# A graph-attention layer on one core: alphas, sums and scores moved one step behind what they need

## The chip, the core and the metric

One core of a Trainium2 chip runs the whole kernel, in one launch. The metric is the device time in microseconds (us), the median of three runs. One further execution was recorded by the hardware profiler; all rows, waits and durations below come from it. Engines are named as in the profile: PE (TensorE matmuls), PEld (TensorE weight loads), DVE (VectorE), ACT (ScalarE), POOL (GpSimd), SP (SyncE, which here only issues DMAs). An engine takes its instructions in the order of the program, and engines wait for each other on semaphores.

## What is computed

There are 12500 nodes with 128 channels and 400000 edges, sorted by their destination. Cut to what matters, and with eight heads of 16 + 16 channels:

```
h       = relu(layernorm(x))
message = (h @ w_src + b_src)[src] + (h @ w_dst)[dst]
rad     = silu(silu(edge_attr @ w1 + b1) @ w2 + b2) @ w3 + b3
message = message * edge_weight * rad
a, v    = heads of message @ w_sep + b_sep          # 8 heads, 16 alphas and 16 values each
score   = sum(smooth_leaky_relu(a) * alpha_dot)     # one number per edge and head
att     = softmax of score over the edges of one destination
out     = x + segment_sum(v * att, dst) @ w_proj + b_proj
```

## The kernel before

**Stages.** A first stage makes the node tables `t_src` and `t_dst` in DRAM (up to L289). The edge stage, `passes`, takes most of the time: 400 steps of 1000 edges, each in two sections of 500 (`f` = 0, 1), in four tiles of 125 edges each. While the last steps drain, and behind them, the sums of sections that share a node are combined (L1012 to L1103); a last stage applies `w_proj` (L1139 to L1192).

**The order is written by hand.** The edge stage stands under a manual schedule: an engine's instructions come in the order in which `step(k)` calls the helpers. One call of `step(k)` works on several steps at once. It starts loads for step k+3 and the gather for k+4, does the radial MLP for k+3 (`e_T`), k+2 (`mlp1`), k+1 (`mlp2`) and k (`mlp3`), makes message k, its alphas and (every second step) its scores, and, 12 steps later (`LAG = 12`, `c = k - LAG`), values and sums of step c. The softmax over eight steps (`softmax_up`, `softmax_down`, `softmax_exp`, `softmax_T`) lies between scores and values.

**The helpers, and their lines in the profile.**

- `gather(k)`: 8 indirect DMAs on POOL, each of which gathers the `t_src` rows of 125 edges into `gs` (L718). `gs` has four buffers, so that the gather for step k+4 waits until message k has read its buffer.
- `mlp3(k)`: PE `p3` (L758), then DVE makes `rad` twice (L761).
- `message(k, rads)`: PE transposes `gs` into `pm` (8 instructions, L770), adds the destinations' rows by a one-hot product (L775), then DVE multiplies by `rad` into `mT` (L779).
- `alphas(k, f)`: PE `pa` (L783), ACT `sl` (L785), DVE `al` (L787).
- `scores(k)`: PE `misc` from the four `al` of two steps (L794), ACT `Sp` (L797), a store to DRAM by SP (L799).
- `sums_begin(c)`: ACT copies the softmax weights into `pvx` (L847), DVE makes the one-hot `oh` (L851, L854).
- `values(c, f)`: PE `V` (L864), DVE `pvx` (L866).
- `sums(c)`: PE `misc` from `oh` and `pvx`, 8 matmuls into two halves of the partitions (L875), ACT copies it to `ob` (L879). `store_win` and `store` (L883, L887) send `ob` to DRAM.
- `mlp1` is L736 and L739, `mlp2` L744 and L746, `e_T` L728 and L730, `softmax_T` L838 and L840.

**PSUM buffers.** All eight banks are in use, most tiles have a single buffer: `misc` is shared by sums, scores, `softmax_T` and `prep_make`; `m1` by `e_T` and `mlp2`; `p3` (two banks) by `mlp1` and `mlp3`; `pa` by the two alphas; `V` by the two values; `pm` has two buffers. A matmul into such a tile waits until the reader of its last content is done.

**The order within a step**, for PE: L758, L770, L775, L864, L783, L864, L736, L744, L783, L875, L728, and every second step L794.

Of the kernel before, what the change touches and what calls it, by code (L numbers as in the profile page):

```python
# [49 lines left out]
PR = 2 * SEC  # L50
MP = 8
MQ = 2 * MP
LAG = 12
EP = 8


# [1 line left out]
def gnn_kernel(ctx: ExitStack, tc: tile.TileContext, a: dict, out: bass.AP):  # L58
# [585 lines left out]
    def passes(w1b, w2b, w3b, b12, w_s, b_s, tgt, far):  # L644
# [5 lines left out]
        with tc.tile_pool(name="wk2", bufs=2) as sp, tc.tile_pool(name="ps", bufs=1, space=PSUM) as pp, \  # L650
# [62 lines left out]
            def gather(k):  # L713
                gs = lp.tile([P, 8, C], F32, name="gs", bufs=4)
                idx, _ = prep[k // 16]
                for j in range(8):
                    t = k % 16 * 8 + j
                    nc.gpsimd.indirect_dma_start(  # L718
                        out=gs[:, j, :], out_offset=None, in_=t_src[:, :],
                        in_offset=bass.IndirectOffsetOnAxis(ap=idx[:, t:t + 1], axis=0))  # L720
                gath[k] = gs
# [10 lines left out]
            def mlp1(k):  # L732
                p1 = pp.tile([P, 2, BANK], F32, name="p3")
                for q in range(2):
                    s = slice(q * 2 * RAD, (q + 1) * 2 * RAD)
                    nc.tensor.matmul(p1[:, q, 0:2 * T], w1b[s, :], eTs[k][s, :],  # L736
                                     start=True, stop=True)
                h1s[k] = sp.tile([P, SEC], F32, name="h1")
                nc.scalar.activation(h1s[k].rearrange("p (q e) -> p q e", q=2), p1[:, :, 0:2 * T],  # L739
                                     AF.Silu, bias=b12[:, 0:1], scale=1.0)  # L740
# [13 lines left out]
            def mlp3(k):  # L754
                p3 = pp.tile([C, 2, BANK], F32, name="p3")
                for f in range(2):
                    s = slice(f * FC, (f + 1) * FC)
                    nc.tensor.matmul(p3[:, f, 0:SEC], w3b[s, :], h2s[k][s, :], start=True, stop=True)  # L758
                rads = [sp.tile([C, SEC], F32, name="rad", bufs=3) for _ in range(2)]
                for f in range(2):  # L760
                    nc.vector.scalar_tensor_tensor(rads[f], p3[:, f, 0:SEC], b3, w_g[k][:, f * SEC:(f + 1) * SEC],  # L761
                                                   op0=ALU.add, op1=ALU.mult)
                return rads

            def message(k, rads):
                gs = gath[k]
                pm = [pp.tile([C, SEC], F32, name="pm", bufs=2) for _ in range(2)]
                for f in range(2):
                    for t in range(TS):
                        nc.tensor.matmul(pm[f][:, t * T:(t + 1) * T], gs[:T, f * TS + t, :],  # L770
                                         ident[:T, :T], start=(t == 0), stop=False,
                                         is_transpose=True, skip_group_check=True)
                for f in range(2):
                    s = slice(f * W, (f + 1) * W)
                    nc.tensor.matmul(pm[f], md[k][s, :], ohT[k][s, :], start=False, stop=True,  # L775
                                     skip_group_check=True)
                mTs[k] = sp.tile([C, PR], F32, name="mT", bufs=LAG + 1)
                for f in range(2):
                    nc.vector.tensor_mul(mTs[k][:, f * SEC:(f + 1) * SEC], pm[f], rads[f])  # L779

            def alphas(k, f):
                pa = pp.tile([C, SEC], F32, name="pa")
                nc.tensor.matmul(pa, w_a, mTs[k][:, f * SEC:(f + 1) * SEC], start=True, stop=True)  # L783
                sl = sp.tile([C, SEC], F32, name="sl")
                nc.scalar.activation(sl, pa, AF.Silu, bias=b_a, scale=1.0)  # L785
                al = sp.tile([C, SEC], F32, name="al", bufs=6)
                nc.vector.scalar_tensor_tensor(al, pa, 0.25, sl, op0=ALU.mult, op1=ALU.add)  # L787
                als[2 * k + f] = al
# [46 lines left out]
            def softmax_T(m):  # L835
                pt = pp.tile([T, TS, P], F32, name="misc")
                for t in range(TS):
                    nc.tensor.transpose(pt[:, t, :], Ps[m][:, t * T:(t + 1) * T], ident)  # L838
                Pem[m] = sp.tile([T, TS, MQ, H], F32, name="Pem")
                nc.scalar.copy(Pem[m].rearrange("p t q h -> p t (q h)"), pt)  # L840


            def sums_begin(c):
                pvx[c] = sp.tile([T, 2, TS, ROW], F32, name="pvx")
                q = c % MP * 2
                for f in range(2):
                    nc.scalar.copy(pvx[c][:, f, :, C:ROW], Pem[c // MP][:, :, q + f, :])  # L847
                _, loc = prep[c // 16]
                ohs[c] = sp.tile([T, 8, W], F32, name="oh")
                t0 = c % 16 * 8  # L850
                nc.vector.tensor_tensor(  # L851
                    ohs[c][:, :, 0:W - 1], lane[:T, 0:W - 1].unsqueeze(1).to_broadcast([T, 8, W - 1]),
                    loc[:, t0:t0 + 8].unsqueeze(2).to_broadcast([T, 8, W - 1]), op=ALU.is_equal)
                nc.vector.tensor_tensor(  # L854
                    ohs[c][:, :, W - 1].rearrange("p (f t) -> p f t", f=2),
                    loc[:, t0:t0 + 8].rearrange("p (f t) -> p f t", f=2),
                    far[:T, 2 * c:2 * c + 2].unsqueeze(2).to_broadcast([T, 2, TS]), op=ALU.is_equal)
# [24 lines left out]
            def store_win(c):  # L882
                nc.sync.dma_start(out=win[c * P:(c + 1) * P, :], in_=accs[c])  # L883

            def store(c, f):
                at = nc.sync.value_load(base[0:1, f, c:c + 1])
                nc.sync.dma_start(out=agg[ds(at, W - 1), :], in_=accs[c][f * W:(f + 1) * W - 1, :])  # L887

            def has(k):
                return 0 <= k < NP  # L890
# [4 lines left out]
                load_e(0, i)  # L895
            def step(k):
                c = k - LAG
                if has(c - 1):
                    store_win(c - 1)
                    store(c - 1, 0)  # L900

                if k % 16 == 4 and has(k + 12):
                    prep_load((k + 12) // 16)
                if has(k + 3):
                    load_w(k + 3)
                    load_md(k + 3)
                if k % 2 and has(k + 3):
                    load_d((k + 3) // 2)
                g, r = divmod(k + 3, EP)
                if k >= -3 and r < EP - 1 and has((g + 1) * EP):  # L910
                    for i in ((0, 1) if r == 0 else (r + 1,)):
                        load_e(g + 1, i)
                if has(k + 4) and (k + 4) % MP == 0:
                    load_sm((k + 4) // MP)
                if has(c - 1):
                    store(c - 1, 1)
                if 0 <= 2 * k < NZ:
                    for i in range(2 * k, min(2 * k + 2, NZ)):
                        zero(i)
                if k % 16 == 8 and has(k + 8):  # L920
                    prep_make((k + 8) // 16)
                if has(k + 4):
                    gather(k + 4)
                if has(c):
                    sums_begin(c)
                if has(k):
                    message(k, mlp3(k))
                if has(c):
                    values(c, 0)
                if has(k):  # L930
                    alphas(k, 0)
                if has(c):
                    values(c, 1)
                if has(k + 2):
                    mlp1(k + 2)
                if has(k + 1):
                    mlp2(k + 1)
                    one_hot_T(k + 1)
                if has(k):
                    alphas(k, 1)  # L940
                if has(c):
                    sums(c)
                m, r = divmod(k, MP)
                if has(k - MP):
                    if r == 1:
                        softmax_up(m - 1)
                    elif r == 2:
                        softmax_down(m - 1)
                        softmax_exp(m - 1)
                    elif r == 3:  # L950
                        softmax_T(m - 1)
                if has(k + 3):
                    e_T(k + 3)
                if has(k) and k % 2 == 1:
                    scores(k)

            for k in range(-5, NP):
                step(k)
# [128 lines left out]
            assert NA == 3 * 4 * P and NE - NA == P // 2  # L1087
            for k in range(NP, NP + LAG + 2):
                step(k)
# [148 lines left out]
```

## Time and profile before

| what | value |
|---|---|
| median of three runs | 6562.58 us (6560.19 to 6575.51) |
| the profiled execution's own time | 6566.2 us |
| its span, first to last instruction | 6564.2 us |
| PE busy | 5066.2 us, 77% |
| POOL busy | 3111.5 us, 47% |
| DVE busy | 2887.1 us, 44% |
| ACT busy | 1785.1 us, 27% |
| mean granted PE clock | 0.873 of full speed |
| first and last L758 | 238.6 and 6296.1 us |
| moved by DMA | 783.25 MB, 119 GB/s over the span |

The 400 steps lie between the two L758 times; outside them are the node stage (about 240 us) and the end (about 270 us). Busy shares are means over work that alternates between two kinds of step, with and without scores, so that the gain or loss of a change is read from one pair of steps in the timeline, not from the shares. The ends of matmuls are modelled by the profiler; when a matmul's result was really there is seen from the instruction on another engine that waited for it.

### The profile page before, as it was taken

How to read it: one execution, taken by the hardware profiler on the slowest of the kernel's cores; microseconds unless marked ns; L12 is line 12 of the kernel's file. 1: busy time of each engine (PE TensorE's matmuls, PEld its weight loads, DVE VectorE, ACT ScalarE, POOL GpSimd, SP SyncE). 2: the span in 40 equal slices, each digit the busy share in tenths (PEclk: the TensorE clock that was granted, in tenths of full speed). 3: DMA queues.
4: the chain of work that ended last, by engine and by line, in shares of the span. 5: the costliest groups of instructions: out<-in, count | busy, mean ns of one | idle time of the engine just before them, and what ended most of it. 6: DMA issues, size and time to landing. Idle time of an engine off the chain costs nothing. (4 is left out here: it accounts for less than half of the span.)

```text
span 6564.2 us, 79188 instructions
## 1 busy us (share of the span) xinstructions
PE 5066.2 (77%) x26490; PEld 2665.6 (41%) x26490; DVE 2887.1 (44%) x5210; ACT 1785.1 (27%) x3797; POOL 3111.5 (47%) x3231
## 2 busy tenths in 40 slices
PE   3477878787878878788788787887887878888774
PEld 2234444444444444444444444444444444444453
DVE  4234444444444444444444444444444444444465
ACT  3122222222222222222222222222222222222221
POOL 0455555455554545544455454454554545545402
PEclk7688898898998989988888898898888989888885
DMA  3454444444444444444444444444444444444423
GB/s 124 135 144 119 124 119 115 125 117 121 121 122 118 121 119 119 124 117 115 123 120 121 119 116 121 122 115 120 121 117 122 119 120 121 124 119 118 114 60 123
DMA packets 884920, 783.25 MB, mean 119 GB/s; under 512 B 527255, under 2 KB 773279, under 8 KB 884250
## 3 DMA queue, kind: packets, MB, share of 16 engines
q1 hardware_dynamic: 778482, 560.72, 31.0%
q0 software_dynamic: 102816, 210.37, 13.6%
q10 hardware_dynamic: 3202, 6.99, 0.3%
q8 instruction: 212, 3.47, 0.2%
q14 instruction: 208, 1.70, 0.1%
HBM read 643.82 MB, written 134.27 MB: 119 GB/s over the span
## 5 line engine op out<-in xcount | busy, mean ns | idle before, releaser
L718 POOL DMA_INDIRECT gs<-t_src,idx x3200 | 3067.4, 959 | 3189.3 <-PE pm L770 1756.2
L787 DVE SCALAR_TENSOR_TENSOR al<-pa,sl 128x500 f32<-128x500 f32 x800 | 542.9, 679 | 1570.9 <-ACT sl L785 1022.1
L761 DVE SCALAR_TENSOR_TENSOR rad<-p,c_fc_b,w_b 128x500 f32<-128x500 f32 x800 | 553.6, 734 | 1389.4 <-PE p L758 1102.0
L783 PE MATMUL pa<-mT,c_w_a 128*128 128x500 f32 x1600 | 833.7, 603 | 256.8 <-DVE mT L779 248.1
L785 ACT ACTIVATE sl<-pa,c_b_a 128x500 f32<-128x500 f32 x800 | 541.4, 677 | 1789.4 <-PE pa L783 626.9
L864 PEld LDWEIGHTS V<-c_w_v,mT 128*125 128x125 f32 x6208 | 741.2, 188 | 634.8 <-issue 337.9
L864 PE MATMUL V<-c_w_v,mT 128*125 128x128 f32 x6208 | 891.3, 286 | 23.2 <-issue 1.1
L794 PE MATMUL misc<-al,w_s 128*32 128x500 f32 x1600 | 365.9, 986 | 539.5 <-ACT ob L879 525.3
L779 DVE TENSOR_TENSOR mT<-pm,rad 128x500 f32<-128x500 f32 x800 | 504.3, 672 | 280.1 <-PE pm L775 252.8
L758 PE MATMUL p<-h,w3b 64*128 64x500 f32 x1600 | 625.5, 870 | 0.0
L770 PEld LDWEIGHTS pm<-ident,gs 125*128 125x128 f32 x3200 | 430.1, 169 | 435.9 <-issue 435.9
L866 DVE TENSOR_TENSOR pvx<-V,Pem 125x512 f32<-125x512 f32 x776 | 528.9, 682 | 44.4 <-PE m L744 26.5
L770 PE MATMUL pm<-ident,gs 125*128 125x125 f32 x3200 | 533.6, 321 | 0.0
L875 PEld LDWEIGHTS misc<-pvx,oh 125*64 125x64 f32 x6400 | 365.5, 137 | 322.4 <-issue 279.7
L875 PE MATMUL misc<-pvx,oh 125*64 125x136 f32 x6400 | 473.0, 287 | 28.2 <-DVE pvx L866 27.6
L783 PEld LDWEIGHTS pa<-mT,c_w_a 128*128 128x128 f32 x1600 | 269.5, 191 | 500.6 <-DVE mT L779 287.4
L775 PE MATMUL pm<-ohT,md 64*128 64x500 f32 x1600 | 471.0, 656 | 0.1
L739 ACT ACTIVATE h<-p,b 128x500 f32<-128x500 f32 x400 | 270.5, 676 | 700.9 <-PE pa L783 157.2
L879 ACT COPY ob<-misc 128x136 f32<-128x136 f32 x400 | 108.7, 272 | 1292.5 <-remote 630.5
L744 PE MATMUL m<-h,w2b 128*128 128x500 f32 x800 | 449.6, 644 | 0.0
L728 PE MATMUL m<-ident,e_t 125*128 125x125 f32 x800 | 187.4, 319 | 204.4 <-ACT h L746 169.8
L746 ACT ACTIVATE h<-m,b 128x500 f32<-128x500 f32 x400 | 270.7, 677 | 223.4 <-PE m L744 55.0
(145 smaller groups left out, 3153.1 us busy)
## 6 DMA issues: line engine op xcount, KB each, us to landing
w_b<-in_edge_weight SPq DMA_DIRECT2D x400, 500.0 KB
d_b<-in_dst SPq DMA_DIRECT2D x400, 250.0 KB
gs<-t_src,idx POOLq DMA_INDIRECT x3200
e_t<-in_edge_attr SPq DMA_DIRECT2D x400, 125.0 KB
sc_d<-Sp SPq DMA_DIRECT2D x200, 250.0 KB
win<-ob SPq DMA_DIRECT2D x400, 68.0 KB
agg<-ob SPq DMA_DIRECT2D x800, 33.5 KB
md<-t_dst SPq DMA_DIRECT2D x800, 32.0 KB
```

The source lines that it names most:

```text
L718: nc.gpsimd.indirect_dma_start(out=gs[:, j, :], out_offset=None, in_=t_src[:, :], in_offset=bass.IndirectOffsetOnAxis(ap=idx[:, t:t + 1], ...
L758: nc.tensor.matmul(p3[:, f, 0:SEC], w3b[s, :], h2s[k][s, :], start=True, stop=True)
L761: nc.vector.scalar_tensor_tensor(rads[f], p3[:, f, 0:SEC], b3, w_g[k][:, f * SEC:(f + 1) * SEC], op0=ALU.add, op1=ALU.mult)
L770: nc.tensor.matmul(pm[f][:, t * T:(t + 1) * T], gs[:T, f * TS + t, :], ident[:T, :T], start=(t == 0), stop=False, is_transpose=True, skip_ ...
L775: nc.tensor.matmul(pm[f], md[k][s, :], ohT[k][s, :], start=False, stop=True, skip_group_check=True)
L779: nc.vector.tensor_mul(mTs[k][:, f * SEC:(f + 1) * SEC], pm[f], rads[f])
L783: nc.tensor.matmul(pa, w_a, mTs[k][:, f * SEC:(f + 1) * SEC], start=True, stop=True)
L785: nc.scalar.activation(sl, pa, AF.Silu, bias=b_a, scale=1.0)
L787: nc.vector.scalar_tensor_tensor(al, pa, 0.25, sl, op0=ALU.mult, op1=ALU.add)
L864: nc.tensor.matmul(V[:, t, :], mTs[c][:, o:o + T], w_v, start=True, stop=True)
L866: nc.vector.tensor_mul(pvx[c][:, f, :, 0:C].rearrange("p t (h k) -> p t h k", h=H), V.rearrange("p t (h k) -> p t h k", h=H), Pem[c // MP] ...
L875: nc.tensor.matmul(acc[f * W:(f + 1) * W, :], ohs[c][:, f * TS + t, :], pvx[c][:, f, t, :], start=(t == 0), stop=(t == TS - 1), skip_group ...
```

## The change

Values, sums, alphas and scores change their places in `step(k)`:

- `LAG` goes from 12 to 13: values of step c come 13 steps after its message. `mT` has `LAG + 1` buffers and so gets one more.
- `alphas(k - 1, f)` instead of `alphas(k, f)`; `scores(k - 1)` at the end of even steps instead of `scores(k)` at the end of odd ones. The softmax helpers run one step later.
- `sums(c - 1)` instead of `sums(c)`, and no longer near the end of the step but between the two alphas, right after the first. The stores of `ob` follow one step later (`c - 2`).
- `sums_begin` is split into `weights` (ACT) and `one_hot` (DVE); the latter moves from the start of the step to its end.
- The first `values` moves ahead of `message`, the second behind `mlp1`.

PE's order within a step becomes: L758, L864, L770, L775, L783, L875, L736, L864, L744, L783, L728, and L794 every second step (lines as before the change).

```diff
-LAG = 12
+LAG = 13
...
-            def sums_begin(c):
+            def weights(c):
                 pvx[c] = sp.tile([T, 2, TS, ROW], F32, name="pvx")
                 q = c % MP * 2
                 for f in range(2):
                     nc.scalar.copy(pvx[c][:, f, :, C:ROW], Pem[c // MP][:, :, q + f, :])
+
+            def one_hot(c):
                 _, loc = prep[c // 16]
                 ohs[c] = sp.tile([T, 8, W], F32, name="oh")
...
-                if has(c - 1):
-                    store_win(c - 1)
-                    store(c - 1, 0)
+                if has(c - 2):
+                    store_win(c - 2)
+                    store(c - 2, 0)
...
-                if has(c - 1):
-                    store(c - 1, 1)
+                if has(c - 2):
+                    store(c - 2, 1)
...
                 if has(k + 4):
                     gather(k + 4)
+
                 if has(c):
-                    sums_begin(c)
-                if has(k):
-                    message(k, mlp3(k))
+                    weights(c)
+                rads = mlp3(k) if has(k) else None
                 if has(c):
                     values(c, 0)
                 if has(k):
-                    alphas(k, 0)
+                    message(k, rads)
+                if has(k - 1):
+                    alphas(k - 1, 0)
+                if has(c - 1):
+                    sums(c - 1)
+                if has(k + 2):
+                    mlp1(k + 2)
                 if has(c):
                     values(c, 1)
-                if has(k + 2):
-                    mlp1(k + 2)
                 if has(k + 1):
                     mlp2(k + 1)
                     one_hot_T(k + 1)
-                if has(k):
-                    alphas(k, 1)
-                if has(c):
-                    sums(c)
+                if has(k - 1):
+                    alphas(k - 1, 1)
                 m, r = divmod(k, MP)
                 if has(k - MP):
-                    if r == 1:
+                    if r == 2:
                         softmax_up(m - 1)
-                    elif r == 2:
+                    elif r == 3:
                         softmax_down(m - 1)
                         softmax_exp(m - 1)
-                    elif r == 3:
+                    elif r == 4:
                         softmax_T(m - 1)
+                if has(c):
+                    one_hot(c)
                 if has(k + 3):
                     e_T(k + 3)
-                if has(k) and k % 2 == 1:
-                    scores(k)
+                if has(k - 1) and k % 2 == 0:
+                    scores(k - 1)
```

## The prediction

> **What bounds the kernel now.** I read the page first. No engine is full, and PE comes nearest:
>
> ```profile
> PE 5066.2 (77%) x26490; PEld 2665.6 (41%) x26490; DVE 2887.1 (44%) x5210; ACT 1785.1 (27%) x3797; POOL 3111.5 (47%) x3231
> ...
> L718 POOL DMA_INDIRECT gs<-t_src,idx x3200 | 3067.4, 959 | 3189.3 <-PE pm L770 1756.2
> ```
>
> Second, the waits of PE (total, times, longest):
>
> ```profile
> PE misc L794 <- ACT ob L879: 525.3, 144, 4.3
> PE pa L783 <- DVE mT L779: 248.1, 169, 19.2
> PE misc L838 <- ACT ob L879: 196.3, 49, 6.5
> PE m L728 <- ACT h L746: 169.8, 103, 8.9
> ```
>
> Three of the four come from this: scores and `softmax_T` wait for the copy of the sums out of `misc`, and alphas for the message of their own step. Third, the timeline of two steps (start, duration, engine, operation, [idle before]):
>
> ```profile
> 3004.23 1.90 PE L794 MATMUL misc<-al,w_s 128*32 128x500 f32 x8 [3.52 <-ACT ob L879]
> 3006.06 2.04 PE L758 MATMUL p<-h,w3b 64*128 64x500 f32 x4
> ...
> 3010.23 0.94 POOL L718 DMA_INDIRECT gs<-t_src,idx  x1 [8.16 <-PE pm L770]
> ...
> 3016.51 1.15 PE L875 MATMUL misc<-pvx,oh 125*64 125x136 f32 x16
> ...
> 3017.95 1.11 PE L758 MATMUL p<-h,w3b 64*128 64x500 f32 x4
> ...
> 3018.96 0.94 POOL L718 DMA_INDIRECT gs<-t_src,idx  x1 [0.30 <-issue]
> ...
> 3021.63 0.27 ACT L879 COPY ob<-misc 128x136 f32<-128x136 f32 x1 [4.34 <-PE pm L775]
> 3021.73 1.38 DVE L761 SCALAR_TENSOR_TENSOR rad<-p,c_fc_b,w_b 128x500 f32<-128x500 f32 x2 [3.06 <-PE pm L775]
> ...
> 3023.76 1.10 PE L783 MATMUL pa<-mT,c_w_a 128*128 128x500 f32 x2 [1.59 <-DVE mT L779]
> ```
>
> The sums end at 3017.66, but ACT, idle, gets them at 3021.63, and DVE gets L758 (end 3019.06) at 3021.73. PE's rows go on at full pace meanwhile: results are there and are reported late, all in one burst. The burst comes 2.7 us after the start of the last of eight gathers, 11.4 us after the first. Next step: last gather 3030.98, `ob` 3033.76. At the end, where no gather runs, sums are reported at once:
>
> ```profile
> 6284.17 1.15 PE L875 MATMUL misc<-pvx,oh 125*64 125x136 f32 x16
> 6285.36 0.27 ACT L879 COPY ob<-misc 128x136 f32<-128x136 f32 x1 [0.41 <-PE misc L875]
> 6285.69 1.05 PE L794 MATMUL misc<-al,w_s 128*32 128x500 f32 x8 [0.37 <-ACT ob L879]
> ```
>
> So sums, 6.3 us behind the first gather, fall into the window (about 7.4 to 11.4 us) in which PE's results wait for POOL. What ends at 0.8 to 2.7 us (L775, L864, the first L783) is read at once, at 4.5 to 6.5 mostly. The idle 3.5 us have a second price, seen in the clock of the stretches before and behind 3010:
>
> ```profile
> 3003.00:3010.00 7.00, 5.77 (x22) 2.37 (x23) 1.38 (x2) 1.44 (x5) 0.00 (x0) 0.51 0.31 83
> 3010.00:3033.70 23.70, 18.38 (x108) 10.09 (x108) 10.93 (x22) 6.19 (x12) 15.09 (x16) 1.00 0.51 132
> ```
>
> Columns six and seven behind the length: at PEclk 0.51 L758 takes 2.04 us, at 1.00 1.11. A pair of steps: 11.9 us without, about 17.8 with scores. From the 12th L758 (427.5) to the 400th (6295.6) 388 steps take 5868 us, 15.12 each.
>
> **The change, part by part.**
>
> *PE's own work* does not change; full clock, start to next start: L758 1.04, L770 1.00, L775 1.04, two L864 2.14, two L783 1.86, L875 1.08, L736 0.62, L744 0.95, L728 0.36: 10.09 us, with scores (0.99 in the end's rows) 11.1; mean with a share of L838 and L680 10.65. This is the floor of a step.
>
> *Alphas of k-1*: L783 no longer waits for this step's `mT`: minus 248 us. What is next late is `pa`, free when the second `al` of the step before is done: sl 0.68 + al 0.68 behind its L783, about 3 us ahead of need. *Sums of c-1* behind the first alphas: `pvx` and `oh` are ready a step earlier, so no wait; they end about 2.8 us behind the first gather instead of 7.4. Behind them on PE stand L736, L864, L744, L783, L728, 4 us of work, before anything wants `misc`: minus 525 and 196 us, as long as the sums are reported by then. *Clock*: with no gap of 3.5 us, L794, L758 and L770 run at full clock (1.90 to 0.99, 1.98 to 1.04, 1.9 to 1.0): 2.8 us per pair.
>
> *Moved for nothing visible*: `one_hot` (DVE 0.84), `weights` (ACT 0.35) and the pvx products: DVE has 6.9 us of work per step, ACT 4.4; if their cover went, `al` behind them would be 0.84 later. Stores of `ob` a step later on SP: SP works 8.1 us per step and loads three steps ahead; the store no longer waits for `ob` (SP waited there 1048 us by its own list). The S load and the softmax keep their distance of two steps. The tail has two more short steps, with 4 us (as at 6303 to 6319) 8 us in sum.
>
> *New waits*: the last L794 needs the `al` made from L783 just ahead of it (0.04 + 0.68 + 0.04 + 0.68 = 1.45 us less L728's 0.36): 1.1 us per pair, hidden before under the 3.5. L728 waits for h of `mlp2` (L746): L744 is 5.4 us behind the first gather, h 0.7 later, L728's turn is at 6.35: no wait; in one step in three or so results at 4.5 to 6.5 us are late by 0.7 to 2 today: I take 0.4 us per step (bounds 0 and 5, when all wait till 11.4).
>
> *The new bound is POOL with the late report*: L758, L864 and L770 of the next step now run in the window of 7.4 to 11.4 us. That L758 is reported at 11.4 costs nothing (rad is wanted by L736 alone, 3 us after). But the next gathers wait for L770: 11.45 + 0.3 = 11.75 us from group to group. With scores: L783 6.35, al 7.8, L794 8.85, L758 9.9, L864 10.95, L770 11.95, gather 12.25. Mean 12.0, plus 0.3 to 0.4 for late reports in the middle: 12.3 per step.
>
> Sum, against the execution's own 6566.2: 388 x (15.12 - 12.3) = 1094 less, 8 more: 5480. The median shown lies 3.6 lower: **5476**. The start's 12 steps, 14.4 us each as their L758 rows have it, are left alone.
>
> **Two rules of the Trainium skill.** Row: sums end at 3017.66, are read at 3021.63. "Perfetto Trace Analysis" (Per-instruction lifecycle, the summary) says that a matmul's end in a profile is an estimate and the true one hidden. By it alone the 4 us could be array work, the floor 14.7, the time 6566 + 8 - 388 x 0.47 = 6390. The rows decide against: PE keeps its pace, and without gathers the lag is 0.05. Second, "TensorE: Matmul & The Clock Gate" (Part 3, The mechanism): matmuls end strictly in program order. It speaks against this change: a late sum holds back all behind it, and now L736, L864, L744, L783 stand behind it, before only L728 and L794. Today's burst shows that order. If sums at 2.8 us are late, it gives the first rival's 7700; the rows at 0.8 to 2.7 us that are never late give 5476.
>
> **The rivals.**
>
> *Slower: it is the sums that wait for the gathers, wherever they stand.* Then mlp2 is known at 11.45, ACT makes ob, h, h (1.7), L728 starts at 13.2, and L758, L864, L770 follow: 17.0 us from group to group; with scores sl, al and L794 come in between: 18.9. Mean 18: 6566 + 8 + 388 x 2.9 = 7700. It decides from a report at about 8.6 us behind the first gather on (8.6 + 5.55 without scores, + 7.45 with, mean 15.1). For: L875 alone is late in every step, while L783 at 7.3 to 7.9 us, in the steps that run a us late, often is not. Against: nothing earlier than 3.8 us is ever late. 0.22, reaching from 6600 to 7900.
>
> *Halfway*: the second L783 or L744 becomes what is held till 11.45. Without scores little changes (11.75), with scores al is ready at 12.9, L770 done at 17.0, gathers at 17.3: mean 14.5, 6333. The same comes out when groups run back to back: in the first 12 steps, where PE has 7 us of work, they do, results are held to the end of both groups (L728 at 394.57 waits 8.93 us), and a step takes 14.4: 6295. For: the window grows with POOL's run. Against: L770 would have to be reported within 7.4 us of the group's start, and PE's 10.65 does not reach that for several steps. 0.18, about 6300, from 5900 to 6540.
>
> *Floor*: no late report hurts: 10.65 per step, 4840. POOL's 10.0 (8 x 1.25) would not forbid it; L770's position does. 0.02. *It does nothing*, because a new wait equals the old: 0.02.
>
> **How the numbers follow.** Main case 0.56, 5150 to 5900 by itself (11.5 to 13.4 per step); halfway 0.18, floor 0.02: faster 0.76. Within 0.3%, about what a measurement of this kernel can tell from no change: 0.02. Slower 0.22. The range from 5050 (11.2 per step, between the floor and the main case) to 7000 leaves out the floor and most of the first rival, 0.17 in all.
>
> **What would show it.** Right: L794 <- ob and L783 <- mT gone from PE's waits; L879 idle-waiting under 0.1 us after L875's end, with L875 ending within 3 us of the first gather; groups of gathers 11.7 to 12.3 us apart; PEclk over 0.95; POOL's wait for L770 down to some 900 us or less. Wrong: L879 again at last gather + 2.7 us, L728 <- L746 in the thousands of us, a clock below 0.85, or groups of gathers running back to back.

## The result: slower, and what the profile shows after

The changed kernel takes 7124.47 us (median of 4 runs, 7093.7 to 7156.7) against 6568.83 of the kernel before: a ratio of 1.085, 95% interval 1.079 to 1.090. The profiled execution has a span of 7091.7 us against 6564.2, so 527.5 us are to be explained. (Lines behind L847 have moved by two: values are now L866, sums L877, the copy of the sums L881.)

The page first. Its rows give PE's busy time, POOL's gathers and the transposes L728 of `e_T` with the idle time ahead of them and what ended it:

```profile
PE 5171.5 (73%) x26490; PEld 2797.8 (39%) x26490; DVE 2936.0 (41%) x5210; ACT 1791.0 (25%) x3797; POOL 3085.4 (44%) x3231
...
L718 POOL DMA_INDIRECT gs<-t_src,idx x3200 | 3042.7, 951 | 3735.9 <-PE pm L770 2643.4
...
L728 PE MATMUL m<-ident,e_t 125*128 125x125 f32 x800 | 228.9, 380 | 1470.4 <-ACT h L746 1285.0
```

PE has the same 26490 matmuls, 105.3 us longer in sum (5171.5 against 5066.2); its idle time is up from 1498.0 to 1920.2, by 422.2. The two make up the 527.5. POOL's wait for L770 has grown from 1756.2 to 2643.4: the groups of gathers start later. The waits of PE say where the idle time is now (total, times, longest):

```profile
PE m L728 <- ACT h L746: 1285.0, 306, 7.7
PE m L728 <- issue: 153.4, 67, 5.3
...
PE misc L794 <- DVE al L787: 44.4, 66, 2.0
...
PE misc L838 <- ACT ob L881: 6.6, 2, 5.9
```

The waits that the change was to remove are gone: L783 for `mT`, L794 for `ob` (525.3), L838 for `ob` (196.3, now 6.6). One has come in their place and is larger than all of them: L728 waits for the h of `mlp2`, because both use the one buffer `m`. The timeline of a step without scores has the mechanism (start, duration, engine, operation, [idle before]; the group's first gather starts at 3014.85, its last at 3023.87):

```profile
3014.85 0.95 POOL L718 DMA_INDIRECT gs<-t_src,idx  x1 [3.58 <-PE pm L770]
...
3016.59 1.15 PE L877 MATMUL misc<-pvx,oh 125*64 125x136 f32 x16
...
3017.66 0.69 PE L736 MATMUL p<-eT,w1b 64*128 64x250 f32 x4
3017.78 0.27 ACT L881 COPY ob<-misc 128x136 f32<-128x136 f32 x1 [0.41 <-PE misc L877]
...
3018.29 1.14 PE L866 MATMUL V<-c_w_v,mT 128*125 128x128 f32 x8
...
3019.16 0.68 ACT L739 ACTIVATE h<-p,b 128x500 f32<-128x500 f32 x1 [1.11 <-PE p L736]
3019.26 1.00 PE L744 MATMUL m<-h,w2b 128*128 128x500 f32 x2
...
3023.54 0.69 DVE L868 TENSOR_TENSOR pvx<-V,Pem 125x512 f32<-125x512 f32 x1 [5.46 <-remote]
...
3023.87 0.94 POOL L718 DMA_INDIRECT gs<-t_src,idx  x1 [0.30 <-issue]
...
3024.25 0.68 ACT L746 ACTIVATE h<-m,b 128x500 f32<-128x500 f32 x1 [4.41 <-remote]
...
3024.98 0.68 PE L728 MATMUL m<-ident,e_t 125*128 125x125 f32 x2 [3.88 <-ACT h L746]
...
3025.59 2.04 PE L758 MATMUL p<-h,w3b 64*128 64x500 f32 x4
...
3028.88 1.02 PE L770 MATMUL pm<-ident,gs 125*128 125x125 f32 x8
...
3030.17 0.95 POOL L718 DMA_INDIRECT gs<-t_src,idx  x1 [5.36 <-PE pm L770]
```

The sums end at 3017.74 and are read at 3017.78: here at once, as forecast. But what stands behind them on PE is read later and later: L736 (end 3018.35) after 0.8 us, the second values L866 (3019.43) after 4.1, L744 (3020.26) after 4.0. ACT and DVE sat idle meanwhile. With h made at 3024.93 only, L728, L758, L866 and L770 follow, and the next group of gathers starts 15.3 us behind the start of this one. The idle 3.9 us are also followed by a half clock, as the 3.5 us were in the kernel before: L758 takes 2.04 us, and only L770 is at full speed again (1.02). The answer by stretches (PE's busy time with its count comes first, the granted clock stands behind the five engines) has 0.99, then 0.72 as the mean of a stretch that is slow at its start:

```profile
3016.00:3025.00 9.00, 5.12 (x35) 2.77 (x33) 2.67 (x5) 2.31 (x4) 6.62 (x7) 0.99 0.76 201
3025.00:3031.00 6.00, 6.00 (x27) 3.32 (x28) 3.27 (x7) 1.17 (x4) 0.83 (x1) 0.72 0.47 101
```

Over the whole run I paired the end of each group of matmuls with the start of its reader, and counted a result as late when the idle reader started more than 0.35 us behind that end. L744 ends 5.4 us behind the first gather after, and 5.5 before: nearly the same place. Before, 108 of 374 were late, by 1.6 us in the median; after, 331 of 374, by 4.6. The sums themselves, at 2.9 us, are late in 331 of 374, but by 0.6 only. Late results in the changed kernel are mostly let through at about 4.2, 5.7, 7.1, 8.5, 9.9 and 11.4 us behind the first gather, so near multiples of 1.42 us, where a group has eight gathers (8 x 1.42 = 11.4). The gathers themselves start 1.25 us apart; what sets the 1.42 is not known. The record of PE's semaphore shows why it looks like a burst: in the kernel before, at 3021.6, a dozen results came through in a row 0.03 to 0.06 us apart, as if a queue were stopped and then emptied in order.

One thing must be known to read the numbers that follow: the kernel before took 6530 to 6642 us on some occasions and 4923 to 4925 us on others. In the kernels traced on the latter, hardly a result of PE was late (some ten in one kernel over 374 steps, none or one in the rest). Each run is therefore compared with the kernel before as it was timed beside it on the same chip. What makes the difference between occasions is not known: the chip that was numbered 1 showed both, though whether it was the same chip both times is not known. The changed kernel itself was timed only where results are late.

### The profile page after: what moved, and what is told of

It reads as the page before. It is cut to its first block, busy times and chain, and to the rows that moved or that the text cites. A ratio compares the mean times of both kernels' runs of the same rounds, so it can differ in the third digit from the quotient of the medians.

```text
span 7091.7 us, 79707 instructions
## 1 busy us (share of the span) xinstructions
PE 5171.5 (73%) x26490; PEld 2797.8 (39%) x26490; DVE 2936.0 (41%) x5210; ACT 1791.0 (25%) x3797; POOL 3085.4 (44%) x3231
## 5 line engine op out<-in xcount | busy, mean ns | idle before, releaser
L718 POOL DMA_INDIRECT gs<-t_src,idx x3200 | 3042.7, 951 | 3735.9 <-PE pm L770 2643.4
L728 PE MATMUL m<-ident,e_t 125*128 125x125 f32 x800 | 228.9, 380 | 1470.4 <-ACT h L746 1285.0
L866 PEld LDWEIGHTS V<-c_w_v,mT 128*125 128x125 f32 x6192 | 887.9, 221 | 575.1 <-issue 306.3
L866 PE MATMUL V<-c_w_v,mT 128*125 128x128 f32 x6192 | 1051.5, 321 | 0.0
L783 PE MATMUL pa<-mT,c_w_a 128*128 128x500 f32 x1600 | 846.5, 611 | 22.6 <-DVE al L787 11.9
L728 PEld LDWEIGHTS m<-ident,e_t 125*128 125x128 f32 x800 | 100.9, 175 | 1763.8 <-ACT h L746 1527.3
L758 PE MATMUL p<-h,w3b 64*128 64x500 f32 x1600 | 662.8, 918 | 0.0
L794 PE MATMUL misc<-al,w_s 128*32 128x500 f32 x1600 | 462.0, 806 | 92.2 <-DVE al L787 44.4
L770 PE MATMUL pm<-ident,gs 125*128 125x125 f32 x3200 | 485.7, 303 | 0.0
L877 PEld LDWEIGHTS misc<-pvx,oh 125*64 125x64 f32 x6400 | 360.4, 137 | 292.7 <-issue 160.1
L783 PEld LDWEIGHTS pa<-mT,c_w_a 128*128 128x128 f32 x1600 | 270.5, 189 | 504.3 <-issue 452.8
L877 PE MATMUL misc<-pvx,oh 125*64 125x136 f32 x6400 | 462.8, 287 | 4.4 <-DVE oh L856 4.0
L770 PEld LDWEIGHTS pm<-ident,gs 125*128 125x128 f32 x3200 | 442.6, 165 | 13.2 <-issue 10.3
L775 PE MATMUL pm<-ohT,md 64*128 64x500 f32 x1600 | 447.4, 636 | 0.0
L744 PE MATMUL m<-h,w2b 128*128 128x500 f32 x800 | 405.7, 589 | 0.0
```

Of the source, the lines that this page charges most:

```text
L718: nc.gpsimd.indirect_dma_start(out=gs[:, j, :], out_offset=None, in_=t_src[:, :], in_offset=bass.IndirectOffsetOnAxis(ap=idx[:, t:t + 1], ...
L794: nc.tensor.matmul(ps[32 * j:32 * j + 32, :], w_s, als.pop(2 * k - 2 + j), start=True, stop=True)
L866: nc.tensor.matmul(V[:, t, :], mTs[c][:, o:o + T], w_v, start=True, stop=True)
L877: nc.tensor.matmul(acc[f * W:(f + 1) * W, :], ohs[c][:, f * TS + t, :], pvx[c][:, f, t, :], start=(t == 0), stop=(t == TS - 1), skip_group ...
```

## The experiments

| kernel | us | before, same chip | late results |
|---|---|---|---|
| after, again | 7110 | 6530 | yes |
| after without gathers | 4945 | 6642 | none |
| before without gathers | 4899 | 6642 | none |
| after, plain load on SP | 4963 | 6642 | none |
| after, sums at the step's end | 6773 | 6642 | yes |
| after, sums ahead of the message | 5675 | 6530 | yes |
| the same | 5134, 5136 | 4924, 4925 | none |
| after, sums in one column group | 7026 / 5348 | 6530 / 4924 | yes / none |
| after, 2 of 16 matmuls of the sums | 5482 / 4728 | 6530 / 4924 | yes / none |
| before, sums alone moved | 5059 | 4925 | none |
| after, four gathers | 4952, 4954 | 4924, 4925 | none |
| reordered | 5900 | 6641 | yes |
| the same | 4768, 4768 | 4925, 4923 | none |

Where no ratio with an interval is given, a time is that of a single execution. In the three kernels without POOL's gathers, "none" is the kernel's own doing (before took 6642 us beside them); in the others it is the occasion's.

**Are the gathers behind the late results?** Both kernels with the gathers of the loop left out:

```diff
                 if has(k + 4):
-                    gather(k + 4)
+                    gather(k + 4) if k < -3 else gath.update({k + 4: gath[0]})
```

> The changed kernel with the gathers of the main loop left out: every step uses the rows gathered for step 0 (so the messages of all later steps are computed from the wrong sources; all other work is done). First theory (results of PE are reported late because POOL's gathers run): nothing is reported late any more, mlp2's h comes 0.1 us behind L744, L728 does not wait, and a step is PE's own work of 10.7 us plus some tenths: about 11.2 us, 4900 to 5200 us in all. Rival (PE's array itself falls behind its rows in the new order, whatever POOL does): lags stay and the time stays at about 7100 us.

> The kernel before with the gathers of the main loop left out in the same way. First theory: the sums are reported at once, L794 <- ob falls from 525 us to some 80 us (0.4 us in every second step), and a step is 11 to 12 us: 5000 to 5400 us in all, near the changed kernel without gathers: the two orders then differ by 200 us at most, and what separates them with gathers is only what each has waiting on a late report. Rival (the old order is better in itself): it stays ahead by some hundred us without gathers too.

Measured: 4945.0 and 4899.0 us on an occasion on which before took 6642.1. The waits for `ob` and for h are gone in both. In the timeline of the changed kernel without gathers L744 ends at 2506.82 and is read at once:

```profile
2505.82 1.00 PE L744 MATMUL m<-h,w2b 128*128 128x500 f32 x2
...
2506.86 0.68 ACT L746 ACTIVATE h<-m,b 128x500 f32<-128x500 f32 x1 [1.22 <-PE m L744]
...
2507.59 0.43 PE L728 MATMUL m<-ident,e_t 125*128 125x125 f32 x2
```

So the gathers are behind it, some 1740 us in the old order and some 2160 in the new (against the 7110 of another occasion), and the two orders themselves differ by 46 us (the new one is the slower by 0.9%). The rival, that the array falls behind by itself in the new order, is out.

**The data that arrives, or POOL's part in the gathers?** The same bytes, as one plain load on SP:

```diff
-                for j in range(8):
-                    ...
-                    nc.gpsimd.indirect_dma_start(
-                    ...
+                nc.sync.dma_start(out=gs, in_=t_src[k % 12 * 1024:k % 12 * 1024 + 1024, :]
+                                  .rearrange("(j p) c -> p j c", p=P))
```

> The changed kernel with each step's eight gathers on POOL replaced by one plain load on SP of as many bytes (1024 rows of the same table in a row, so that the messages come from the wrong sources; all other work is done). If POOL's own making of the gathers holds the reports: as without gathers, 4900 to 5400 us, lags under 0.2 us. If the arriving data (0.5 MB a step into SBUF) holds them: 6500 to 7100 us, with late reports while the loads land.

```profile
gs<-t_src SPq DMA_DIRECT2D x400, 512.0 KB
```

The page's list of issues has 512 KB per step through SP, and the time is 4962.9 us, 18 more than without any gather. 0.5 MB arriving a step holds nothing up; it is the indirect gathers issued by POOL that do. Whether it is POOL's part in them or their scattered rows was not taken apart, since this load reads its rows in sequence.

**One part undone: the sums back at the step's end.**

```diff
                 if has(c):
                     weights(c)
+                    one_hot(c)
...
-                if has(c - 1):
-                    sums(c - 1)
...
                     alphas(k - 1, 1)
+                if has(c):
+                    sums(c)
...
-                if has(c):
-                    one_hot(c)
```

(The stores of `ob` come a step earlier again, too.)

> The changed kernel with one part undone: the sums go back to the step's end, behind the second alphas, with their own step's values (one_hot back at the start, stores of c-1); alphas, scores and the softmax stay a step behind, the first values stay ahead of the message, the second behind mlp1. If the sums' new place, early in the run of gathers, is what makes the results behind it late: L744's h is late in a third of the steps as in the kernel before, L728's wait falls from 1285 to about 200 us, the sums are held to 11.4 us behind the first gather again, and the time is 6400 to 6650 us. If the other moves are to blame: about 7100 us, and L728 still waits for over 1000 us.

```profile
PE misc L794 <- ACT ob L881: 624.0, 128, 6.3
PE misc L838 <- ACT ob L881: 218.5, 49, 5.4
```

6772.7 us against 6642.1, a fiftieth over before, and outside the expected 6400 to 6650: the old waits for `ob` are back and L728's for h is down to 42.6 us. L744 is late in 78 of 374 steps. The sums, at 6.2 us, are late in 368 of 375, by 5.3 us. So the sums' new place makes most of the loss. The other parts together cost 131 us here, of the 556 to 580 us that the whole change cost beside its own kernel before; which of them it is stays open.

**What stands behind the sums.** The sums moved ahead of the message, between two groups of gathers:

```diff
                 if has(c):
                     values(c, 0)
+                if has(c - 1):
+                    sums(c - 1)
                 if has(k):
                     message(k, rads)
                 if has(k - 1):
                     alphas(k - 1, 0)
-                if has(c - 1):
-                    sums(c - 1)
```

> The changed kernel with the sums moved once more: still of the step before (c-1) and still with alphas and scores a step behind, but ahead of the message, so that they run when the gathers of the step before are over or nearly so and the next have not begun. Theory A (inside a run of gathers it is the sums that start the late reporting, and everything behind them is let through late): L736, L744 and L783 are read at once or in a third of the steps late, L728 <- L746 falls from 1285 to under 200 us, groups of gathers follow each other after 12 to 13 us, and the time is 5300 to 5800 us, far below both kernels. Theory B (whatever ends later than some 3 us behind the first gather is late, the sums are nothing special): L744 at 4.3 us is late as often as in the changed kernel and the time stays at 6700 to 7100 us.

This first run fell on an occasion without late results (5134.2 against 4924.0). The next one did not, and had the changed kernel beside it:

> The changed kernel as it is, beside the kernel before on the same chip. Two chips have shown two times for the kernel before: 6642 us, with late reports, and 4924 us, with none at all in four other kernels. Where before takes about 6600, this takes about 7100 and L744's h is late in most steps. Where before takes about 4920, no result is late, and the changed kernel takes 4900 to 5000 us, as it does without gathers (4945): then the change is worth plus or minus 50 us there, and its loss is nothing but waits for late reports.

> The changed kernel with the sums ahead of the message, again (5134 us on a chip where nothing was late). On a chip with late reports: theory A (the sums start them, inside a run of gathers) 5300 to 5900 us and L744 late in under a third of the steps; theory B (all that ends later than 3 us is late, whatever stands before it) 6700 to 7100 us with L744 late in most steps. On a chip without: 5134 again.

The changed kernel took 7109.9, with the sums first 5674.6, before 6530.3: the new order without the sums' place is 13% faster than before, in single executions. Its waits of PE, and four lines of its timeline:

```profile
PE misc L877 <- ACT Sp L797: 95.9, 70, 2.8
PE m L728 <- ACT h L746: 76.2, 31, 9.2
```

```profile
3020.07 0.95 POOL L718 DMA_INDIRECT gs<-t_src,idx  x1 [2.37 <-PE pm L770]
...
3023.31 1.00 PE L744 MATMUL m<-h,w2b 128*128 128x500 f32 x2
...
3024.35 0.68 ACT L746 ACTIVATE h<-m,b 128x500 f32<-128x500 f32 x1 [1.22 <-PE m L744]
...
3025.09 0.43 PE L728 MATMUL m<-ident,e_t 125*128 125x125 f32 x2
```

L744 ends 4.2 us behind the first gather and is read 0.04 us later; it is late in 29 of 374 steps, where it was in 359 of 374 in the changed kernel beside it. Theory B (later than 3 us is late) falls. The sums and L758 are late now, let through at 11.4 to 11.6 us in the median, but little except the next gathers needs them: groups follow each other after 12.2 us in the median, 12.9 in the mean. The 12.3 of the prediction is near this order's median and 0.6 under its mean, far from what the changed kernel does.

L744 also ends a us earlier here than in the changed kernel (4.1 us in the median), so that place and time change together. One group of matmuls separates them: L736 ends 3 to 4 us behind the first gather in 368 steps of the changed kernel, right behind the sums, and is late in 271 of them; it ends there in 192 steps of the reordered kernel (the last one below), with no sums ahead of it, and is late in none.

The same order a third time:

> The sums ahead of the message, timed in rounds (5675 us in one look beside 6530 of before; 5134 beside 4924 on a chip where nothing was late). Theory A: 0.86 to 0.88 of before where results are late, 1.03 to 1.05 where not. If the one look was a lucky state: over 6000 us.

On an occasion without late results: 5136.4, a ratio of 1.043 (1.041 to 1.045). This order is good against late results and bad without them.

**What of the sums does it?** Same columns of the array for both halves, then two matmuls of the sixteen:

```diff
-                acc = pp.tile([P, ROW], F32, name="misc")
-                for t in range(TS):
-                    for f in range(2):
-                        nc.tensor.matmul(acc[f * W:(f + 1) * W, :], ohs[c][:, f * TS + t, :],
...
+                acc = pp.tile([W, 2, ROW], F32, name="misc")
+                for f in range(2):
+                    for t in range(TS):
+                        nc.tensor.matmul(acc[:, f, :], ohs[c][:, f * TS + t, :],
...
-                nc.scalar.copy(ob, acc)
+                for f in range(2):
+                    nc.scalar.copy(ob[f * W:(f + 1) * W, :], acc[:, f, :])
```

> The changed kernel with the sums of both halves written to the same 64 partitions of PSUM (two ranges of one bank), so that all 16 matmuls use the same columns of the array instead of the halves by turns; two copies take the place of one on ACT (some 0.25 us a step more there). If the use of two column groups by turns is what starts the late reporting: 5300 to 6200 us and L744 late in under a third of the steps. If the number of matmuls or their time is: as the changed kernel, 6900 to 7200 us.

> The changed kernel with the sums of both halves in the same 64 columns of the array, again (5348 us on a chip where nothing was late; there the sums took 2.0 us instead of 1.1). On a chip with late reports: if the two column groups by turns start them, 5350 to 5900 us; if the number of matmuls does, 7000 to 7500 us. On a chip without: 5348 again.

```diff
-                for t in range(TS):
+                for t in range(1):
...
-                                         pvx[c][:, f, t, :], start=(t == 0), stop=(t == TS - 1),
+                                         pvx[c][:, f, t, :], start=True, stop=True,
```

> The changed kernel with 2 of the 16 matmuls of the sums left (one tile of each half instead of four, so the sums are of a quarter of the edges); their place and what waits for them stay. Theory A with the sums' mass of small matmuls as the trigger: little is late behind them, L744 in under a third of the steps, and the time falls to 5300 to 6000 us (PE's work alone would give 0.95 us a step, 370 us). If any sums in this place start it (their form, or simply PE's results at this time): 6500 to 7000 us, L728 still waits for over 800 us.

> The changed kernel with 2 of the 16 matmuls of the sums, again (4728 us on a chip where nothing was late). On a chip with late reports: if the mass of the sums starts them, 4800 to 5600 us, L744 late in under a third of the steps; if whatever stands at this place does, 6500 to 7000 us. On a chip without: 4728 again.

With late results: 7026.2 us for the one column group, though its sums take 367 us more of PE, and 5481.5 for the two matmuls, of which some 280 us are work left out (L877's rows fall from 462.8 to 182.0 us). The waits for h, of the one and of the other:

```profile
PE m L728 <- ACT h L746: 1055.1, 333, 6.3
```

```profile
PE p L736 <- DVE rad L761: 159.6, 121, 11.1
PE m L728 <- ACT h L746: 97.9, 43, 10.2
```

L744 is late in 372 of 374 steps with sixteen matmuls in one column group, in 54 of 374 with two. So the turns between column groups are not it. The two matmuls are no clean test of the number, though. With them L744 ends at 3.4 us behind the first gather in the median, not at 5.4, and in 227 steps the sums end before the first gather starts (19 of these late); in the other 147 they lie within the gathers, and L744, at 4.0 us, is late in 35. Whether the number of the matmuls, their weight loads, the time that they take or their place among the gathers decides is open. Without late results the two took 5348.4 and 4728.2.

**Two that stayed inconclusive.** Half the gathers, and the sums moved in the kernel before by themselves:

```diff
-                for j in range(8):
+                for j in range(4):
...
-                        nc.tensor.matmul(pm[f][:, t * T:(t + 1) * T], gs[:T, f * TS + t, :],
+                        nc.tensor.matmul(pm[f][:, t * T:(t + 1) * T], gs[:T, t, :],
```

> The changed kernel with four gathers a step instead of eight (both halves of a step read the rows of the first: half of the messages come from the wrong sources; all other work is done). If each gather holds the reports for 1.42 us and the burst comes at the end of the last: the latest releases move from 11.4 to 5.7 us behind the first gather, L744 is known at 5.7, nothing waits for it any longer, and the step is PE's work, 11 to 11.5 us: 4900 to 5300 us. If the delay goes with the sums and not with the length of the gathers: L728 <- L746 stays over 800 us and the time over 6300 us.

> The changed kernel with four gathers a step instead of eight (half of the messages come from the wrong sources), again (4952 us on the chip where nothing was late). If each gather holds the reports for 1.42 us: nothing is released later than 5.8 us behind the first gather of a group of four, and the time falls to 4950 to 5400 us. If the delay belongs to the sums and not to the number of gathers: 6000 us and more.

```diff
                     alphas(k, 0)
+                if has(c - 1):
+                    sums(c - 1)
                 if has(c):
                     values(c, 1)
...
-                if has(c):
-                    sums(c)
```

(The stores of `ob` come a step later, too.)

> The kernel before with one part of the change alone: the sums, of the step before (c-1), move between the first alphas and the second values; all else (alphas, scores, values, lag) stays as before. Theory A: this alone starts the loss: L744's h is late in most steps, L728 <- L746 takes over 800 us, 6900 to 7400 us. Rival (the loss needs the alphas or scores a step behind): 6000 to 6600 us, since L794 <- ob (525 us) is gone. On a chip where nothing is late: 4900 to 5050 us.

All three runs fell on occasions without late results (4952.0, 4953.6 and 5059.0 us), where they say nothing on the question. The first two are the nearest that there is to the changed kernel on such an occasion: 0.6% over before, with half the gathers. That each gather stands for 1.42 us of the delay is therefore read from the traces, not tested by a change of their number.

**An order for all of it.** All that is wanted within the step ahead of the sums:

```diff
                 if has(k):
                     message(k, rads)
+                if has(k - 2) and k % 2 == 1:
+                    scores(k - 2)
+                if has(k + 1):
+                    mlp2(k + 1)
+                    one_hot_T(k + 1)
                 if has(k - 1):
                     alphas(k - 1, 0)
-                if has(c - 1):
-                    sums(c - 1)
...
-                if has(k + 1):
-                    mlp2(k + 1)
-                    one_hot_T(k + 1)
...
-                if has(k - 1) and k % 2 == 0:
-                    scores(k - 1)
+                if has(c - 1):
+                    sums(c - 1)
```

> The changed kernel with all that is wanted within the step put ahead of the sums: scores (of steps k-3 and k-2, in odd steps) and mlp2 right behind the message, the sums last in the step. Theory A (the sums start the late reporting, and only what stands behind them pays): L744 ends some 2 us behind the first gather and is read at once, L728 <- L746 falls under 100 us, the sums are released at 11.4 us with nobody waiting, groups of gathers 11.8 to 12.6 us apart: 5350 to 5650 us against 6530 to 6640 of before, also below the sums-first order (5675). Rival (another result takes their place: V ahead of L770, or the second alphas, late to 11.4 us): 5900 to 6600 us. On a chip where nothing is late: 4850 to 5100 us, PE's work.

> The order with scores and mlp2 right behind the message and the sums last, again (4768 us, 0.969 of before, on the chip where nothing is late). On a chip with late reports: theory A 5350 to 5650 us, 0.82 to 0.86 of before, L744 read at once, groups of gathers 11.8 to 12.6 us apart; rival (V ahead of L770 or the second alphas become what is late) 5900 to 6600 us. On a chip without: 0.967 to 0.970 again.

> The order with scores and mlp2 right behind the message and the sums last, again (0.969 of before on the chip where nothing is late). On a chip with late reports: theory A 5350 to 5650 us, 0.82 to 0.86 of before; rival (V ahead of L770 or the second alphas become what is late) 5900 to 6600 us. On a chip without: 0.967 to 0.972 again.

Without late results twice 0.969 and 0.970 of before (0.967 to 0.970 and 0.968 to 0.972). With them 5899.8 us, 0.889 of before (0.884 to 0.894): faster on both kinds of occasion, the only order with all its work for which that was measured, but 250 us over the range of theory A and at the rim of its rival's. Its waits of PE with late results:

```profile
PE pm L770 <- issue: 253.8, 381, 1.9
PE misc L877 <- ACT Pem L840: 154.7, 30, 7.6
PE misc L680 <- ACT ob L881: 84.7, 17, 5.7
...
PE V L866 <- DVE pvx L868: 59.9, 33, 4.3
```

L728's wait for h is down to 4.1 us and L744 is late in 3 of 374 steps, as expected. But the sums, now last, share `misc` with `softmax_T` (L838) of every eighth step: its copy L840 waits for a late result, the sums for the copy, and such a step takes 18.6 us in the median from gathers to gathers, where the median of all is 12.4. Every sixteenth step `prep_make` (L680) waits for the copy of the sums in the same way (18.5 us). The same fault as that of the change, in a place that I had not considered. By an estimate from these steps (50 of the one kind, 4.8 us over the median in the mean, and 25 of the other, 6.0 over), the two cost nearly 400 us. The first wait on the list names no releaser, and what it stands for is open.

The rival was right in part. The second values, at 4.8 us and ahead of the sums, are late in 264 of 374 steps (by 1.6 us in the median), and the second alphas in 283 (by 2.0), though little waits for them; a step of this kernel has both:

```profile
2896.80 0.96 POOL L718 DMA_INDIRECT gs<-t_src,idx  x1 [2.49 <-PE pm L775]
...
2900.56 1.14 PE L866 MATMUL V<-c_w_v,mT 128*125 128x128 f32 x8
...
2901.53 1.06 PE L783 MATMUL pa<-mT,c_w_a 128*128 128x500 f32 x2
...
2902.74 1.15 PE L877 MATMUL misc<-pvx,oh 125*64 125x136 f32 x16
...
2903.36 0.69 DVE L868 TENSOR_TENSOR pvx<-V,Pem 125x512 f32<-125x512 f32 x1 [1.92 <-PE m L728]
...
2904.09 0.68 ACT L785 ACTIVATE sl<-pa,c_b_a 128x500 f32<-128x500 f32 x1 [2.74 <-PE misc L877]
```

Within this group of gathers the sums (L877) stand behind the two, and still the second values (end 2901.70) are read 1.7 us late and the second alphas (2902.59) 1.5. So theory A does not hold as it was put: the sums make what stands behind them late earlier and more often, but late results start without them too.

## Why the prediction was wrong, by its own steps

- *L783 for `mT`, L794 and L838 for `ob` go*: right. 525.3, 248.1 and 196.3 us are off PE's waits or down to 6.6.
- *The sums, ended 2.8 us behind the first gather, are reported by the time `misc` is wanted*: right, though not within the 0.1 us named as a sign. They end at 2.9 and are late by 0.6 us.
- *L728 waits for h: 0.4 us per step, bounds 0 and 5*: this is the term that failed. L728's two waits, 1285.0 and 153.4, are 3.7 us for each of the 387 steps behind the start. The sum of 12.3 us per step lacks 3.3 us here; with 16.56 measured from the 13th L758 (409.3) to the 400th (6819.6), 1.0 is left, and the half clock behind the wait is of that size (L758 2.04 for 1.11 us). What misled me: I took lateness as a matter of the time behind the first gather, and read off the kernel before how often a result at 4.5 to 6.5 us is late. That share was true with the sums behind L744. With the sums ahead of it, at nearly the same place (5.4 us, not 5.5), it is 331 of 374 and not 108. Nor does it carry over that next to nothing before 3.8 us was late: L736, at 3.5 us, is late in 271 of 368 steps.
- *Clock over 0.95*: wrong for the same reason, 0.841, since the idle time moved from L794 to L728 and the half clock with it.
- *Groups of gathers 11.7 to 12.3 us apart*: wrong here, 17.7 in the median; right (12.2) in the order with the sums ahead of the message, where nothing wanted at once stands behind them.
- *The first rival (7700, sums held until 11.45)*: right in sign, in its range (6600 to 7900) and in the wait that it names (L728 on h), wrong on what is held. The sums are let through early; those behind them are not, so that L744's result, where it is late, comes at 10.0 us in the median and h 0.7 later, not at 11.45 or more. Its break-even, a report at 8.6 us, fits roughly: 10.0 is 1.4 later, and a step went from 15.16 to 16.56. (The prediction's "12th L758" at 427.5 is the 13th, so its 15.12 is 15.16; and its 14.4 us for each step of the start leaves out the first, 15.7 with it.)
- *The two rules of the Trainium skill.* "TensorE: Matmul & The Clock Gate" (Part 3, The mechanism), matmuls end strictly in program order, was set aside because nothing at 0.8 to 2.7 us was ever late. The rows agree (L736, L866 and L744 end at 3018.35, 3019.43 and 3020.26, and are read in that order). The page speaks of the ends and not of their reports; what the runs add is that what stands behind a late result is late too, and four groups that had stood ahead of the sums (L736, the second values, L744, the second L783) now stand behind them. Its price of 7700 was too high, since the delay grows from group to group and does not begin with its full length. "Perfetto Trace Analysis" (Per-instruction lifecycle, the summary), the end of a matmul is an estimate, did not bear on it: without gathers the reader starts 0.04 us behind the modelled end.
- *Halfway (6300) and floor (4840)*: neither came. The floor's mechanism, no late report, is what the kernel without gathers shows: 4945 us.

## What to carry to other kernels

When a result is read late, ask not only when it ends but what stands ahead of it in its queue: a group of instructions that is moved forward to spare its own reader can make everyone late whom it now precedes, and a share of late results that was measured in the old order does not hold in the new. Before moving a group, list which readers behind it hold back the same engine within the step (here through one shared buffer, `m`). And a kernel that owes a quarter of its time to such delays can rank its versions in opposite order on another occasion, so the version to keep is the one that wins on both.

## What was not expected of the hardware

- Indirect gathers issued by POOL held back results of PE that the same bytes through SP did not: 7110 us against 4963 for the same order of work, on two occasions on which the kernel before took 6530 and 6642.
- That was so on some occasions only: the same kernel took 6530 to 6642 us or 4923 to 4925 us, and the gathers on POOL ran in both (0.95 us each, eight in 8.7 us from first start to last).
- Results of the same matmuls (L736), at the same 3 to 4 us behind the first gather, were late in 271 of 368 steps behind sixteen small matmuls, in none of 192 without them ahead; the two halves of the array's columns by turns or not made little difference (L744 late in 331 to 372 of 374 steps). Later in the run, results were late without them too (264 of 374 at 4.8 us). Why is open.
